# Gate products of a graph network in blocks: seven block multiplications in place of eight

## The chip, the cores and the metric

One core of one Trainium2 chip. The metric is the device time of one execution in microseconds (us), median. Executions of one kernel agree within about 0.2%. Ratios are the mean time of one kernel's fast runs over that of the kernel before in the same rounds, so they are not quite the ratio of the medians that are quoted.

## The reference

64 graphs of 256 nodes with 256 features, f32. Layer 0 is a normalisation with ReLU and three rounds of message passing with a gated (GRU) update; layer 1 is a graph attention. Cut to what matters:

```python
for i in range(3):
    m = h @ weight[i]
    aggr = A^T m                                # per graph
    gi = aggr @ w_ih.T + b_ih                   # three gates of 256 from 256
    gh = h    @ w_hh.T + b_hh
    r = sigmoid(i_r + h_r);  z = sigmoid(i_z + h_z)
    n = tanh(i_n + r * h_n)
    h = (1 - z) * n + z * h
x = x + h
# then, per graph: h1 = relu(norm(x)) @ W.T ; masked softmax of scores ; x = x + alpha @ h1
```

## The kernel before

Two graphs (a "pair") are worked on together, features on partitions, so that a gate operand is 2 x 128 features by 2 x 256 nodes = 512 columns. The products `weight[i] @ w_ih.T` are formed once (`gw`). A gate block of 128 outputs is then 2 or 4 multiplications of 128x128 by 128x512 into one result bank of PSUM:

```python
def gate(e, parts, ...):
    pg = Buf("bank")
    for part in parts:                 # "h": hidden state, "i": aggregate
        for kb in range(DB):           # two halves of the contraction
            w = whhT[:, kb, ts(e, P)] if part == "h" else gw[:, i, kb, ts(e, P)]
            nc.tensor.matmul(pg.t, w, feats(src)[:, kb, :], start=..., stop=...)
    ...
```

PSUM is the memory that TensorE writes its results to; SBUF is the working memory that all engines share. That makes 8 for r, 8 for z and 8 for n per layer: 24 wide multiplications. ScalarE applies sigmoid and tanh, VectorE the elementwise rest. The attention ends with a handover: TensorE transposes the softmax weights into PSUM ("turn"), VectorE copies them to SBUF, and TensorE multiplies ("mix"):

```python
pe(4 * TR, turn, ...)                                            # transposes
dve(V512, lambda: nc.vector.tensor_copy(pT.t[:, :GN], pt.t), ...)
pe(4 * MM, mix, ...)                                             # alpha @ h1
```

Every call of `pe`, `act`, `dve`, `pool` adds an operation with an assumed duration to a plan. A list scheduler in the kernel orders them: at each step it takes the operation that can start earliest by the assumed durations, then the one with the nearest deadline. At most three pairs are under way, and the deadline of pair p is 78 us x p in this kernel. The order that it finds is fixed for each engine; at run time an engine works through its own in sequence.

## Time and profile before

Median 2653.11 us (2652.37 to 2654.27). Busy shares of the span:

| engine | busy us | share |
|---|---|---|
| TensorE (PE) | 2613.3 | 99% |
| VectorE (DVE) | 1141.7 | 43% |
| ScalarE (ACT) | 1021.2 | 39% |
| GpSimd (POOL) | 251.0 | 9% |

A busy share is an upper bound on useful work: matmuls overlap, their ends are modelled, and the tail of one covers a short wait behind it. The cost of a matmul is its distance to the next start. In the page's groups the columns are the line, engine and operation, what is written and read, the shapes and the count, then busy us, mean ns of one, and idle time before it with its releaser. PE is TensorE's multiplications and PEld its weight loads, which are instructions of their own.

One more thing is seen in the chain in order of time (start us, length us, what). These are the first gate stretches of two pairs in a row:

```profile
228.03 20.85 PE bank L427 x48
...
309.07 20.84 PE bank L427 x48
```

A pair takes 309.07 - 228.03 = 81.04 us (81.03 over several).

### The profile page before, as it was taken

To read this page: it belongs to the slowest core of one execution; us is meant where nothing else is said; L and a number is where in the kernel's file an instruction comes from. 1 tells how busy PE (TensorE), PEld (TensorE's weight loads), DVE (VectorE), ACT (ScalarE), POOL (GpSimd) and SP (SyncE) were. 2 spreads that over 40 slices of the span, in tenths; PEclk is the share of its full clock that TensorE was granted. 3 is DMA by queue.
4 is the path that set the end of the run, shared out by engine and by line. 5 is a ranking of instruction groups with operands and counts; after the bars stand their busy time and mean duration, and the time that the engine had idled before them with its cause. 6 is when DMAs were issued, how large, how long until landed. Compare 5 with 4: busy or idle time off the path is not lost.

```text
span 2652.0 us, 23413 instructions
## 1 busy us (share of the span) xinstructions
PE 2613.3 (99%) x8929; PEld 1442.7 (54%) x8929; DVE 1141.7 (43%) x2341; ACT 1021.2 (39%) x1885; POOL 251.0 (9%) x294
## 2 busy tenths in 40 slices
PE   8999999999999999999999999999999999999997
PEld 5555555555555555555555545555555555455554
DVE  2444544344443445443444434354434444343433
ACT  3434443234443344432344433444323444334432
POOL 2101110101100011101011000111010110001000
PEclk9999999999999999999999999999999999999998
DMA  3000000000000000000000000000000000000000
GB/s 111 8 24 25 24 24 0 24 24 24 24 9 16 24 24 24 24 1 24 24 24 24 9 15 24 24 24 24 1 24 24 24 25 9 16 8 9 8 9 8
DMA packets 53520, 54.46 MB, mean 21 GB/s; under 512 B 1680, under 2 KB 53408, under 8 KB 53408
## 3 DMA queue, kind: packets, MB, share of 16 engines
q1 hardware_dynamic: 53376, 52.96, 6.0%
q8 instruction: 70, 1.15, 0.2%
q14 instruction: 42, 0.34, 0.0%
q10 hardware_dynamic: 32, 0.01, 0.0%
HBM read 36.18 MB, written 16.78 MB: 20 GB/s over the span
## 4 chain that ended last, share of the span: by engine, by line
PE 98%; DVE 1%; ACT 0%; DMA 0%; issue 0%; POOL 0%; ACTq 0%; DVEq 0%
PE bank L427 75%; PE bank L410 7%; PE bank L556 4%; PE bank L501 4%; PE bank L473 3%; PE bank L372 2%; DVE full L551 1%; PE bank L547 1%; PE bank L307 1%; PE bank L512 0%; PE bank L284 0%; DMA rows<-in_L_gnn_b_hh_dram 0%; ACT full L531 0%; DVE small L344 0%; ACT L531 0%
## 5 line engine op out<-in xcount | busy, mean ns | idle before, releaser
L427 PE MATMUL bank<-full,whhT 128*128 128x512 f32 x2304 | 1032.0, 593 | 0.0
L427 PE MATMUL bank<-full,gw 128*128 128x512 f32 x2304 | 1028.6, 593 | 0.0
L427 PEld LDWEIGHTS bank<-full,gw 128*128 128x128 f32 x2304 | 428.2, 190 | 515.1 <-issue 491.7
L427 PEld LDWEIGHTS bank<-full,whhT 128*128 128x128 f32 x2304 | 426.0, 190 | 474.2 <-issue 473.2
L444 DVE SCALAR_TENSOR_TENSOR full<-bank,vec,full 128x512 f32<-128x512 f32 x192 | 141.4, 749 | 562.2 <-ACT full L441 394.4
L449 ACT ACTIVATE full<-full,vec 128x512 f32<-128x512 f32 x192 | 138.5, 722 | 604.8 <-DVE full L448 604.8
L352 POOL TENSOR_TENSOR small<-small,nhalf 128x2 f32<-128x2 f32 x128 | 102.9, 821 | 2310.8 <-DVE small L350 2310.8
L448 DVE TENSOR_TENSOR full<-full,bank 128x512 f32<-128x512 f32 x192 | 131.3, 684 | 428.5 <-PE bank L427 428.5
L359 ACT ACTIVATE full<-x,small 128x256 f32<-128x256 f32 x256 | 139.3, 594 | 273.6 <-DVE small L354 273.6
L441 ACT ACTIVATE full<-bank,b_rz 128x512 f32<-128x512 f32 x192 | 131.9, 687 | 257.5 <-PE bank L427 257.5
L410 PE MATMUL bank<-round,round 128*128 128x256 f32 x1536 | 229.0, 302 | 0.0
L410 PEld LDWEIGHTS bank<-round,round 128*128 128x128 f32 x1536 | 195.6, 191 | 31.1 <-issue 30.6
L455 DVE TENSOR_TENSOR full<-full,full 128x512 f32<-128x512 f32 x192 | 132.5, 690 | 126.1 <-ACT full L449 126.1
L414 ACT COPY full<-bank 128x512 f32<-128x512 f32 x192 | 109.3, 589 | 154.2 <-PE bank L410 154.2
L452 ACT ACTIVATE full<-bank,b_rz 128x512 f32<-128x512 f32 x192 | 131.9, 687 | 71.6 <-PE bank L427 71.2
L457 DVE TENSOR_TENSOR full<-full,full 128x512 f32<-128x512 f32 x192 | 132.3, 689 | 20.1 <-ACT full L452 20.1
L458 DVE TENSOR_TENSOR full<-full,full 128x512 f32<-128x512 f32 x192 | 132.8, 692 | 6.6
L556 PE MATMUL bank<-full,full 128*128 128x256 f32 x512 | 119.6, 386 | 10.3 <-DVE full L551 10.3
L481 ACT CAST round<-bank 128x512 fp32r<-128x512 f32 x128 | 68.8, 589 | 153.5 <-PE bank L473 153.5
L501 PE MATMUL bank<-wT,full 128*128 128x258 f32 x512 | 117.8, 382 | 0.0
L483 DVE TENSOR_TENSOR round<-bank,round 128x512 fp32r<-128x512 f32 x128 | 81.6, 679 | 75.0 <-ACT round L481 75.0
L473 PEld LDWEIGHTS bank<-ident,full 128*128 128x128 f32 x768 | 90.9, 142 | 42.0 <-issue 34.6
(54 smaller groups left out, 1522.2 us busy)
## 6 DMA issues: line engine op xcount, KB each, us to landing
x<-in_x_dram SPq DMA_DIRECT2D x32, 512.0 KB, 4.8
adj<-in_adj_dram SPq DMA_DIRECT2D x32, 512.0 KB, 3.9
out_dram<-x SPq DMA_DIRECT2D x32, 512.0 KB, 2.8
full<-in_L_gnn_w_ih_dram SPq DMA_DIRECT2D x2, 384.0 KB, 5.9
full<-in_L_gnn_w_hh_dram SPq DMA_DIRECT2D x2, 384.0 KB, 6.8
full<-in_L_gnn_weight_dram SPq DMA_DIRECT2D x3, 256.0 KB, 6.6
full<-in_L_gnn_W_dram SPq DMA_DIRECT2D x1, 256.0 KB, 7.1
rows<-in_L_gnn_a_dram ACTq DMA_DIRECT2D x1, 2.0 KB
```

The source lines that it names most:

```text
L359: act(495, lambda k=k, nb=nb: nc.scalar.activation(nodes(dst)[:, k, :], nodes(src)[:, k, :], AF.Relu, bias=sm.t[:, 18 + nb : 19 + nb], sca ...
L410: nc.tensor.matmul(pa.t[:, ts(db, N)], nodes(part)[:, k, ts(db, P)], Ar()[:, k, :], start=(n == 0), stop=(n == len(terms) - 1))
L427: nc.tensor.matmul(pg.t, w, feats(src)[:, kb, :], start=(part == parts[0] and kb == 0), stop=(part == parts[-1] and kb == DB - 1))
L441: act(AB512, lambda pr=pr, ub=ub, er=er: nc.scalar.activation(ub(), pr.t, AF.Sigmoid, bias=b_rz[:, er : er + 1]), r=[(pr, ONE), ("b_rz", O ...
L444: dve(665, lambda ph=ph, ub=ub, en=en: nc.vector.scalar_tensor_tensor(ub(), ph.t, b_h[:, en : en + 1], ub(), op0=ALU.add, op1=ALU.mult), r ...
L449: act(630, lambda ub=ub, en=en: nc.scalar.activation(ub(), ub(), AF.Tanh, bias=b_i[:, en : en + 1]), r=[("vec", ONE)], w=[(u, q)])
L455: dve(V512, lambda d=d, ub=ub, db=db, hT=hT: nc.vector.tensor_sub(d(), feats(hT)[:, db, :], ub()), r=[(hT, q), (u, q)], w=[(hT_new, q)])
L457: dve(V512, lambda d=d, zb=zb: nc.vector.tensor_mul(d(), d(), zb()), r=[(z, q)], w=[(hT_new, q)])
L458: dve(V512, lambda d=d, ub=ub: nc.vector.tensor_add(d(), d(), ub()), r=[(u, q)], w=[(hT_new, q)])
L473: nc.tensor.transpose(pt.t[:, (nb * DB + db) * P : (nb * DB + db + 1) * P], feats(hT)[:, db, ts(g * NB + nb, P)], ident)
L501: nc.tensor.matmul(pm.t[:, : D + 2], quarters(hT)[:, db, g, ts(nb, P)], wT[:, db, :], start=(db == 0), stop=(db == DB - 1))
L556: nc.tensor.matmul(pv.t[:, ts(ib, D)], pT.t[:, (jb * NB + ib) * P : (jb * NB + ib + 1) * P], h1v()[:, g * NB + jb, :D], start=(jb == 0), s ...
```

## The change

The intent is to take TensorE work away. Weight and operand are each split into 2x2 blocks (output half by feature half; feature half by graph). The seven-product scheme replaces the eight block multiplications: with A the weight and B the operand,

S1 = A21+A22, S2 = S1-A11, S3 = A11-A21, S4 = A12-S2; T1 = B12-B11, T2 = B22-T1, T3 = B22-B12, T4 = T2-B21.

The weight sums are formed once in the setup (F11, F12, FS1 to FS4 in the code; FM22 is minus A22). The operand's sums are formed in each layer, on GpSimd for the hidden state and on VectorE for the aggregate. Three result banks X, Q, Z collect the products. X goes on accumulating after ScalarE has copied it out ("snapshot"), and VectorE adds Q or Z to the copies. Core of the diff, cut:

```diff
-    plan.slot_class("full", [... for i in range(20)])
+    plan.slot_class("full", [... for i in range(23)])
-    plan.slot_class("x", [... for i in range(WINDOW + 2)])
+    plan.slot_class("x", [... for i in range(WINDOW + 1)])
...
+        for sel in ("hh", "g"):
+            product(X, F11, ("B", B11), sel)
+            product(Q, F12, ("B", B21), sel)
+            product(Z, FS1, ("T", T1), sel)
+        snap(0, 0)                       # ScalarE copies X
+        add(0, 0, Q)                     # VectorE adds bank Q to the copy
+        ... product(X, FS2, ("T", T2), sel)
+        snap(0, 1)
+        ... product(X, FS3, ("T", T3), sel)
+        snap(1, 1)
+        add(1, 1, Z)
+        ... product(X, FM22, ("T", T4), sel);  product(Z, FS4, ("B", B22), sel)
+        add(0, 1, Z)
+        return X                         # X itself is the fourth block
...
+            Th = right_factors(nc.gpsimd, pool, hT)
+            Tg = right_factors(nc.vector, dve, agT)
+            Xrz = block_product([gates(0), gates(1)], RZ)
+            Xn = block_product([gates(2)[:1], gates(2)[1:]], U)
...
-        order = plan.run(lambda p: 78000.0 * max(p, 0))
+        order = plan.run(lambda p: 30000.0 * max(p, 0))
```

The last line makes the deadlines flatter, 30 us from pair to pair, so the scheduler mixes the pairs under way more freely.

More of the change, by code (lines that the diff above doesn't have):

```diff
@@ L185, in tile_gated_gnn_then_gat @@
     WIDE = NBLK * (D + 2)
-    plan.slot_class("full", [const.tile([P, WIDE], F32, name=f"full{i}") for i in range(20)])
+    plan.slot_class("full", [const.tile([P, WIDE], F32, name=f"full{i}") for i in range(23)])
     plan.slot_class("round", [const.tile([P, NBLK * D], F32R, name=f"round{i}") for i in range(9)])
-    plan.slot_class("x", [const.tile([P, NBLK * D], F32, name=f"x{i}") for i in range(WINDOW + 2)])
+    plan.slot_class("x", [const.tile([P, NBLK * D], F32, name=f"x{i}") for i in range(WINDOW + 1)])
     plan.slot_class("adj", [const.tile([P, NBLK * N], I32, name=f"adj{i}") for i in range(2)])
@@ L231, in tile_gated_gnn_then_gat @@
     b_h = vec[:, 2 * DB + EB :]
-    gw = const.tile([P, L, DB, E3], F32, name="gw")
-    whhT = const.tile([P, DB, E3], F32, name="whhT")
+    F11, F12, FS4, FM22, FS1, FS2, FS3 = range(7)
+    fac = {m: const.tile([P, 7, 3, P], F32, name=f"fac_{m}") for m in ("hh", 0, 1, 2)}
     wT = const.tile([P, DB, D + 2], F32, name="wT")
@@ L288, in transposed, with factors, sums, copies @@
                         dst(c)[:, r0 * P : (r0 + n) * P], pt.t[:, : n * P]), r=[(pt, ONE)], w=[region(c, r0)])
+        def factors(m, T):
+            blk = lambda eb, kb: T[kb].t[:, :E3].rearrange("p (s b e) -> p s b e", s=3, b=DB)[:, :, eb, :]
+            f = fac[m]
+            def sums():
+                nc.vector.tensor_add(f[:, FS1], blk(1, 0), blk(1, 1))
+                nc.vector.tensor_sub(f[:, FS2], f[:, FS1], blk(0, 0))
+                nc.vector.tensor_sub(f[:, FS3], blk(0, 0), blk(1, 0))
+                nc.vector.tensor_sub(f[:, FS4], blk(0, 1), f[:, FS2])
+                nc.vector.tensor_scalar(f[:, FM22], blk(1, 1), -1.0, None, op0=ALU.mult)
+            def copies():
+                nc.scalar.copy(f[:, F11], blk(0, 0))
+                nc.scalar.copy(f[:, F12], blk(0, 1))
+            r = [(T[kb], (0, 3)) for kb in range(DB)]
+            act(900, copies, r=r, w=[(f"fac{m}", (0,))])
+            dve(2200, sums, r=r, w=[(f"fac{m}", (1,))])
         whh_n = rows_of(w_hh, EB)
         load(0)
-        transposed(lambda c: whhT[:, c, :], lambda c, r0: ("whhT", ((c, r0),)), whh_n)
+        whhT = [Buf("full") for _ in range(DB)]
+        transposed(lambda c: whhT[c].t, lambda c, r0: (whhT[c], (r0,)), whh_n)
+        factors("hh", whhT)
         wih_n = rows_of(w_ih, EB)
@@ L299, in setup @@
             transposed(lambda c, w_T=w_T: feats(w_T)[:, c, :], lambda c, r0, w_T=w_T: (w_T, ((c, r0),)), w_n)
+            gT = [Buf("full") for _ in range(DB)]
             for db in range(DB):
@@ L310, in setup @@
                     pe(3 * MM, go, r=[(w_T, ((0, 0), (1, 0))), (wihT[0], (0, 3)), (wihT[1], (0, 3))], w=[(pg, ONE)])
-                    act(370, lambda i=i, db=db, sl=sl, pg=pg: nc.scalar.copy(gw[:, i, db, sl], pg.t[:, : E3 // 2]),
-                        r=[(pg, ONE)], w=[("gw", ((i, db, half),))])
+                    act(370, lambda b=gT[db], sl=sl, pg=pg: nc.scalar.copy(b.t[:, sl], pg.t[:, : E3 // 2]),
+                        r=[(pg, ONE)], w=[(gT[db], (3 * half,))])
+            factors(i, gT)
         W_n = rows_of(W, DB)
@@ L327, in setup, with right_factors, first @@
                 r=[(pl, ONE)], w=[("wT", (DB + db,))])
-    WHH = [("whhT", tuple((c, r0) for c in range(DB) for r0 in (0, 3)))]
     WT = [("wT", (0, 1, 2, 3))]
-    def gw_keys(i, e):
-        return [("gw", tuple((i, db, e // 3) for db in range(DB)))]
+    B11, B12, B21, B22 = range(4)
+    T1, T3, T2, T4 = range(4)
+    quarter = lambda b, q: b.t[:, q * N : (q + 1) * N]
+    def right_factors(eng, op, b):
+        T = Buf("full")
+        c = (1195, 605, 605) if eng is nc.gpsimd else (V512, V256, V256)
+        def first():
+            q = quarters(b)
+            eng.tensor_sub(T.t[:, : 2 * N].rearrange("p (c n) -> p c n", c=2), q[:, :, 1, :],
+                           b.t[:, : 2 * N].rearrange("p (c n) -> p c n", c=2))
+        op(c[0], first, r=[(b, (B11, B12, B22))], w=[(T, (T1, T3))])
+        op(c[1], lambda: eng.tensor_sub(quarter(T, T2), quarter(b, B22), quarter(T, T1)),
+           r=[(b, (B22,)), (T, (T1,))], w=[(T, (T2,))])
+        op(c[2], lambda: eng.tensor_sub(quarter(T, T4), quarter(T, T2), quarter(b, B21)),
+           r=[(b, (B21,)), (T, (T2,))], w=[(T, (T4,))])
+        return T
@@ new lines, in block_product, with product, go, snap @@
+    def block_product(halves, dest):
+        X, Q, Z = Buf("bank"), Buf("bank"), Buf("bank")
+        both = lambda b: b.t.rearrange("p (s n) -> p s n", s=2)
+        started = set()
+        def product(bank, f, right, sel):
+            terms = [(s, t) for s in range(2) for t in halves[s] if t[0] == sel or (sel == "g" and t[0] != "hh")]
+            if not terms:
+                return
+            first = bank not in started
+            started.add(bank)
+            kind, q = right
+            srcs = lambda t: t[2] if kind == "B" else t[3]
+            def go():
+                for n, (s, t) in enumerate(terms):
+                    nc.tensor.matmul(bank.t[:, ts(s, N)], fac[t[0]][:, f, t[1], :], quarter(srcs(t), q),
+                                     start=(first and n == 0), stop=True, skip_group_check=True)
+            pe(MM * len(terms), go, r=[(srcs(t), (q,)) for _, t in terms] + [(f"fac{t[0]}", (0, 1)) for _, t in terms],
+               w=[(bank, ONE)])
+        def snap(e, g):
+            act(A512, lambda: nc.scalar.copy(quarters(dest[e])[:, :, g, :], both(X)), r=[(X, ONE)], w=[(dest[e], (g, 2 + g))])
+        def add(e, g, bank):
+            dve(V512, lambda: nc.vector.tensor_add(quarters(dest[e])[:, :, g, :], quarters(dest[e])[:, :, g, :], both(bank)),
+                r=[(bank, ONE)], w=[(dest[e], (g, 2 + g))])
+        for sel in ("hh", "g"):
[4 more added lines that the diff above has]
+        add(0, 0, Q)
+        for sel in ("hh", "g"):
+            product(X, FS2, ("T", T2), sel)
+        snap(0, 1)
+        for sel in ("hh", "g"):
+            product(X, FS3, ("T", T3), sel)
+        snap(1, 1)
+        add(1, 1, Z)
+        for sel in ("hh", "g"):
+            product(X, FM22, ("T", T4), sel)
+            product(Z, FS4, ("B", B22), sel)
+        add(0, 1, Z)
+        return X
@@ L416, in pair @@
                     r=[(pa, ONE)], w=[(agT, (g, G + g))])
-            def gate(e, parts, i=i, hT=hT, agT=agT):
-                pg = Buf("bank")
-                for part in parts:
-                    src = hT if part == "h" else agT
-                    def go(part=part, src=src):
-                        for kb in range(DB):
-                            w = whhT[:, kb, ts(e, P)] if part == "h" else gw[:, i, kb, ts(e, P)]
-                            nc.tensor.matmul(pg.t, w, feats(src)[:, kb, :],
-                                             start=(part == parts[0] and kb == 0),
-                                             stop=(part == parts[-1] and kb == DB - 1))
-                    pe(4 * MM, go, r=[(src, ALL)] + (WHH if part == "h" else gw_keys(i, e)), w=[(pg, ONE)])
-                return pg
@@ L434, in pair @@
-            hT_new, u, z = Buf("full"), Buf("full"), Buf("full")
+            Tg = right_factors(nc.vector, dve, agT)
+            RZ, U = [Buf("full") for _ in range(DB)], [Buf("full") for _ in range(DB)]
+            gates = lambda s: [("hh", s, hT, Th), (i, s, agT, Tg)]
+            Xrz = block_product([gates(0), gates(1)], RZ)
+            Xn = block_product([gates(2)[:1], gates(2)[1:]], U)
+            act(A512, lambda U=U, Xn=Xn: nc.scalar.copy(quarters(U[1])[:, :, 0, :], Xn.t.rearrange("p (s n) -> p s n", s=2)),
+                r=[(Xn, ONE)], w=[(U[1], (0, 2))])
@@ new lines, in pair @@
+            for s in range(2):
+                act(630, lambda s=s, RZ=RZ: nc.scalar.activation(
+                    feats(RZ[0])[:, s, :], feats(RZ[0])[:, s, :], AF.Sigmoid, bias=b_rz[:, 2 * s : 2 * s + 1]),
+                    r=[("b_rz", ONE)], w=[(RZ[0], (2 * s, 2 * s + 1))])
+                act(370, lambda s=s, RZ=RZ, X=Xrz: nc.scalar.activation(
+                    quarter(RZ[1], 2 * s), X.t[:, ts(s, N)], AF.Sigmoid, bias=b_rz[:, 2 * s + 1 : 2 * s + 2]),
+                    r=[("b_rz", ONE), (Xrz, ONE)], w=[(RZ[1], (2 * s,))])
+                act(370, lambda s=s, RZ=RZ: nc.scalar.activation(
+                    quarter(RZ[1], 2 * s + 1), quarter(RZ[1], 2 * s + 1), AF.Sigmoid, bias=b_rz[:, 2 * s + 1 : 2 * s + 2]),
+                    r=[("b_rz", ONE)], w=[(RZ[1], (2 * s + 1,))])
@@ L435, in pair @@
             for db in range(DB):
-                er, ez, en = db, DB + db, 2 * DB + db
+                en = 2 * DB + db
+                u = lambda b=U[db]: feats(b)[:, 0, :]
+                d = lambda db=db, hT=hT: feats(hT)[:, db, :]
                 q = (2 * db, 2 * db + 1)
-                ub = lambda db=db, u=u: feats(u)[:, db, :]
-                zb = lambda db=db, z=z: feats(z)[:, db, :]
-                pr = gate(er, "hi")
-                act(AB512, lambda pr=pr, ub=ub, er=er: nc.scalar.activation(
-                    ub(), pr.t, AF.Sigmoid, bias=b_rz[:, er : er + 1]), r=[(pr, ONE), ("b_rz", ONE)], w=[(u, q)])
@@ L443, in pair @@
-                ph = gate(en, "h")
-                dve(665, lambda ph=ph, ub=ub, en=en: nc.vector.scalar_tensor_tensor(
-                    ub(), ph.t, b_h[:, en : en + 1], ub(), op0=ALU.add, op1=ALU.mult),
-                    r=[(ph, ONE), ("vec", ONE)], w=[(u, q)])
-                pn = gate(en, "i")
-                dve(V512, lambda pn=pn, ub=ub: nc.vector.tensor_add(ub(), ub(), pn.t), r=[(pn, ONE)], w=[(u, q)])
-                act(630, lambda ub=ub, en=en: nc.scalar.activation(
-                    ub(), ub(), AF.Tanh, bias=b_i[:, en : en + 1]), r=[("vec", ONE)], w=[(u, q)])
@@ L451, in pair @@
-                pz = gate(ez, "hi")
-                act(AB512, lambda pz=pz, zb=zb, ez=ez: nc.scalar.activation(
-                    zb(), pz.t, AF.Sigmoid, bias=b_rz[:, ez : ez + 1]), r=[(pz, ONE), ("b_rz", ONE)], w=[(z, q)])
-                d = lambda db=db, b=hT_new: feats(b)[:, db, :]
-                dve(V512, lambda d=d, ub=ub, db=db, hT=hT: nc.vector.tensor_sub(d(), feats(hT)[:, db, :], ub()),
-                    r=[(hT, q), (u, q)], w=[(hT_new, q)])
-                dve(V512, lambda d=d, zb=zb: nc.vector.tensor_mul(d(), d(), zb()), r=[(z, q)], w=[(hT_new, q)])
@@ L458, in pair @@
-                dve(V512, lambda d=d, ub=ub: nc.vector.tensor_add(d(), d(), ub()), r=[(u, q)], w=[(hT_new, q)])
-            hT = hT_new
+                dve(660, lambda u=u, db=db, en=en, RZ=RZ: nc.vector.scalar_tensor_tensor(
+                    u(), u(), b_h[:, en : en + 1], feats(RZ[db])[:, 0, :], op0=ALU.add, op1=ALU.mult),
+                    r=[(RZ[db], (0, 1)), ("vec", ONE)], w=[(U[db], (0, 1))])
+                dve(V512, lambda u=u, b=U[db]: nc.vector.tensor_add(u(), u(), feats(b)[:, 1, :]),
+                    r=[(U[db], (2, 3))], w=[(U[db], (0, 1))])
@@ new lines, in pair @@
+                act(630, lambda u=u, en=en: nc.scalar.activation(u(), u(), AF.Tanh, bias=b_i[:, en : en + 1]),
+                    r=[("vec", ONE)], w=[(U[db], (0, 1))])
+                dve(V512, lambda u=u, d=d: nc.vector.tensor_sub(d(), d(), u()), r=[(U[db], (0, 1))], w=[(hT, q)])
+                dve(V512, lambda d=d, b=RZ[db]: nc.vector.tensor_mul(d(), d(), feats(b)[:, 1, :]),
+                    r=[(RZ[db], (2, 3))], w=[(hT, q)])
+                dve(V512, lambda u=u, d=d: nc.vector.tensor_add(d(), d(), u()), r=[(U[db], (0, 1))], w=[(hT, q)])
```

## The prediction

> **What bounds the kernel now.** I read the page first: the busy shares, the 40 slices, the chain that ended last and the costliest groups. The chain in order of time came next, then the busy time by stretches and single rows of the timeline.
>
> ```profile
> PE 2613.3 (99%) x8929; PEld 1442.7 (54%) x8929; DVE 1141.7 (43%) x2341; ACT 1021.2 (39%) x1885; POOL 251.0 (9%) x294
> PE 98%; DVE 1%; ACT 0%; DMA 0%; issue 0%; POOL 0%; ACTq 0%; DVEq 0%
> L427 PE MATMUL bank<-full,whhT 128*128 128x512 f32 x2304 | 1032.0, 593 | 0.0
> L427 PE MATMUL bank<-full,gw 128*128 128x512 f32 x2304 | 1028.6, 593 | 0.0
> ...
> L448 DVE TENSOR_TENSOR full<-full,bank 128x512 f32<-128x512 f32 x192 | 131.3, 684 | 428.5 <-PE bank L427 428.5
> ```
>
> TensorE sets the end: 98% of the chain lies on it, and the three other compute engines are idle for more than half of the span. The gate products (L427) are 4608 instructions. The program has 24 multiplications per layer and pair of graphs, times 96, which is 2304: each f32 multiplication is two instructions. Their mean of 593 ns is a latency, not a cost, since neighbours overlap. The cost is start to start, which the chain in order of time gives:
>
> ```profile
> 147.26 20.60 PE bank L427 x48
> 174.08 20.60 PE bank L427 x48
> ...
> 1248.01 0.87 PE bank L473 x8
> 1248.88 6.87 PE bank L427 x16
> ...
> 1258.34 3.49 PE bank L501 x16
> ...
> 1268.30 1.91 PE bank L410 x16
> ```
>
> Wide gate instruction (512 columns): 20.60/48 = 429.2 ns. The projection has 258 columns, f32, with a fresh weight load each: 3.49/16 = 218.1 ns. So 256 columns should take about 216.5 ns, and one load per 216 ns is hidden. A transpose is 0.87/8 = 109 ns, a propagation 1.91/16 = 119 ns. This pace gives the gates 4608 x 0.4292 = 1978 us; all of TensorE's work at such paces sums to about 2596 us, so about 56 us of the span is idle or drain. Where that is:
>
> ```profile
> 0.00:66.00 66.00, 55.54 (x200) 33.06 (x201) 16.43 (x44) 25.80 (x50) 14.59 (x21) 1.00 0.33 112
> 66.00:2500.00 2434.00, 2423.91 (x8314) 1337.36 (x8313) 1067.73 (x2189) 947.71 (x1746) 233.72 (x269) 1.00 0.06 19
> 2500.00:2571.00 71.00, 69.46 (x219) 36.46 (x218) 30.64 (x57) 25.34 (x46) 1.34 (x2) 1.00 0.00 1
> 2571.00:2652.00 81.00, 64.37 (x201) 35.85 (x198) 26.86 (x52) 22.38 (x43) 1.34 (x2) 0.89 0.04 13
> ```
>
> (First number the length, second TensorE's busy time.) The ramp loses 10 us, the long middle only 10 us in 2434, the last 81 us about 17. The rest of the 56 is drain that counts as busy. The steady state is wholly bound by TensorE.
>
> **What the Trainium skill says.** "TensorE: Matmul & The Clock Gate", section Back-to-back issue gap, gives N/2.4 + 2.5 ns for a warm matmul. The trace agrees if each f32 instruction makes two passes: 2 x 512/2.4 + 2.5 = 429.2, exactly what is seen, and 2 x 258/2.4 + 2.5 = 217.5 against 218.1. So halving the columns costs almost nothing per column here: two narrow instructions take 433.0 against 429.2. "PSUM — Partial Sum Buffer", section The four PSUM rules, says that hardware allows a synchronised read of a partial sum in the middle of an accumulation group; the change rests on it, and no trace of the kernel before shows it. "VectorE: DVE Perf Modes", section The TRN2 errata, gives (N+151)/0.96 ns for an f32 two-tensor operation: 691 at 512, as measured (medians of 692 on L455, L457 and L458), and so 424 at 256. "SBUF — State Buffer", section 🔬 SBUF: two separate sides, says that VectorE with two SBUF inputs and GpSimd lock each other out for a whole instruction. L396 on GpSimd reads 1265/1270/1300 ns min/median/max, so there was no such collision before; there can be now.
>
> **The change part by part**, per layer and pair (96 of them).
>
> Removed from TensorE: 24 wide multiplications become 6 products x 7 x 256 columns = 42 narrow ones; the built order confirms 4032 of them in all. 42 x 2 x 0.2165 = 18.19 us against 24 x 2 x 0.4292 = 20.60. Saved 2.41 us, x96 = 232 us. If nothing else moved, the time would be 2653 - 232 = 2421 us.
>
> Added on VectorE: six additions from PSUM at 684 ns (4.10 us) and the sums of the aggregated operand, one of 512 columns and two of 256 (0.69 + 2 x 0.42 = 1.54). 5.64 x 96 = 542 us, and about 11 us of weight sums in the setup. 1142 becomes 1695, which is 69% of a span of 2450.
>
> Added on ScalarE: seven snapshots and copies out of PSUM at 589 ns (the L414 kind): 4.12 us. The four sigmoids of 687 ns (2.75 us) become two from SBUF at about 722, two half-width from PSUM at about 475 and two half-width from SBUF at 498: 3.39. Sum 4.76 x 96 = 457 us; 1021 becomes 1478, 60%.
>
> Added on GpSimd: sums of the hidden state, 1.27 + about 2 x 0.64 = 2.55, x96 = 245 us; 251 becomes 496, 20%.
>
> None of the additions is TensorE's own work, and no engine rises above TensorE's 96%. What of it reaches the path is waits. A result bank is read by ScalarE and then accumulated further, so the next multiplication into it has to wait for the snapshot. After the last multiplication of a group that is 0.16 us of drain beyond its slot, 0.59 us of copy and two handovers of 0.05 (0.04 to 0.05 in the timeline): about 0.86 us, if ScalarE is free. In the built order I counted the TensorE work laid between the two accesses for the 429 places that show a ScalarE wait on a bank in mid-use: at least 0.96 us, 1.7 us or more in 335, median 2.2. So the order covers every snapshot, but 94 have at most some 0.8 us to spare, and ScalarE, 60% busy in strict order, will sometimes be late. I charge 0.1 us for each of the 672 snapshots and copies: 67 us if none of it is absorbed; I take half to three quarters, 30 to 50 us, an estimate and not a measurement.
>
> Ramp: the weight products now come ahead of the first gate work, and each set needs two copies (2 x 0.48) and five sums of 384 columns (5 x 0.56 = 2.8, from the VectorE formula). I charge 5 us over the old 10. Tail: before, the last pair runs its last two layers alone. The new order interleaves the last pairs more closely (products of two pairs alternate until about the last layer), which should return a few us, while the lone last layer now has a longer chain of snapshots and additions. I set it to zero net. The x buffers fall from 5 to 4 and the general ones rise from 20 to 23; the inputs land in about 5 us and are asked for two pairs ahead, so I charge nothing.
>
> Sum: 2653 - 232 + 5 + 24 to 44 = 2450 to 2470; I choose 2455.
>
> **The rivals.** (1) Waits for the snapshots and additions eat most of the gain: three banks per block product, up to two products per pair-layer, in eight banks with several pairs alive. For it: 69% and 60% busy engines working in strict order, and more waits in TensorE's order (1705 rows carry one against 1358). Against it: the spacing of 0.96 us or more, and that the same kind of static order lost only 0.4% in the middle of the kernel before. If each of the 672 cost 0.3 us, 200 us would come back and the time would be about 2620. (2) GpSimd and VectorE lock each other out: 8.5 us of two-input SBUF work per layer on VectorE against 2.55 us on GpSimd. For it: the skill's page. Against it: both have idle time, and an overlap chance of about a third x 2.55 us is under 1 us per layer and mostly off TensorE's path. It would add 0 to 40 us. (3) Weight loads show up: twice as many loads per streamed column. Against it: 218.1 ns at 258 columns with a load each. If they cost 10 ns each, 8064 x 0.010 = 81 us, a time of about 2530. (4) The waits vanish altogether and the closer interleaving also hides the old waits: TensorE's new work is 2596 - 232 = 2364, plus 40 of ramp and tail, about 2405.
>
> **Range and chances.** The floor of the range is rival 4, the top is rival 3 or half of rival 1: 2405 to 2530. Faster by over 2% means under 2600; only a full rival 1 or two rivals together miss it. Faster 0.94, within 2% 0.05, slower 0.01.
>
> **What would show it.** Right: 8064 gate instructions at about 216 ns start to start, PE busy near 2400 us, VectorE near 1700, ScalarE near 1480, GpSimd near 500, the chain still above 90% on TensorE, and idle before the gate products of some tens of us, released by ScalarE. Wrong: a pace of 225 ns or more (rival 3); chain shares on ScalarE or VectorE of 5% and up, or idle of over 100 us before the gate matmuls (rival 1); GpSimd sums well above 1.3 us or VectorE's two-input rows above 692 ns (rival 2). A busy sum of VectorE far above 1700 would mean that I missed work.

## The result, and the profile after

Median 2404.19 us (2403.07 to 2405.30, four runs) against 2652.74 in the same rounds: ratio 0.9062, 95% interval 0.9046 to 0.9078. That is just under the lower end of the predicted range (2405) and 51 us under the predicted 2455. From the page after, its busy line and the share of the chain by engine:

```profile
PE 2366.8 (99%) x12385; PEld 2097.8 (87%) x12385; DVE 1671.0 (70%) x3225; ACT 1412.9 (59%) x2757; POOL 536.2 (22%) x582
PE 96%; DVE 2%; ACT 1%; issue 0%; DMA 0%; POOL 0%; ACTq 0%; DVEq 0%; POOLq 0%
```

TensorE still sets the end. The added busy time of the others is near what the prediction worked out (1695, 1478 and 496). The chain in order of time, after, two successive pairs:

```profile
199.01 11.22 PE bank L404 x52
214.30 5.61 PE bank L404 x26
...
271.81 11.22 PE bank L404 x52
```

A 256-column gate instruction is 5.61/26 = 215.8 ns start to start, and a pair takes 271.81 - 199.01 = 72.80 us. The idle time before the gate products, by releaser (us in all, times). This view adds the wait of a weight load to that of the multiplication behind it, although the two overlap:

```profile
its engine sat idle before it (us, times) until:
  DVE full L552: 7.3, 4
  ACT full L411: 2.6, 2
  DVE full L376: 0.4, 2
```

So of the 2.6 us for the 576 snapshots (L411), 1.5 are one weight load's wait and 1.1 that of the multiplication behind it, in one place: TensorE waited for a snapshot once. Ramp, middle and tail after (length, then TensorE's busy time):

```profile
0.00:66.00 66.00, 55.54 (x265) 44.23 (x266) 31.49 (x69) 33.91 (x68) 22.06 (x29) 0.97 0.32 104
66.00:2320.00 2254.00, 2250.78 (x11845) 2004.22 (x11844) 1594.68 (x3066) 1342.03 (x2613) 508.66 (x546) 1.00 0.06 21
2320.00:2402.30 82.30, 60.51 (x279) 49.32 (x277) 44.87 (x92) 36.95 (x78) 5.44 (x7) 0.87 0.04 13
```

The ramp idles as long as before (10.5 us), the middle 3 us of 2254, the tail 22 of 82 us (17 of 81 before).

**Where 250 us went.** Thirty-two pairs at the old period are 2593.0 us of a span of 2652.0; at the new one they are 2329.6 of 2402.3. So the periods gave 263.4 us and the ramp and tail took back 13.7. Of the 263.4, the gate products are 4608 x 0.4292 - 8064 x 0.2158 = 237.5 us. The other 25.9 us, 0.8 per pair, are not in the pace of the products. The chain shows most of it at the handover to the mix. Before:

```profile
216.88 0.45 PE bank L547 x4
217.33 0.02 issue
217.35 0.70 DVE full L551
218.05 0.04 issue
218.10 3.72 PE bank L556 x16
```

The chain leaves TensorE for VectorE's copy, and the mix itself takes 3.72 us. After:

```profile
248.65 0.87 PE bank L640 x8
249.52 0.43 PE bank L404 x2
249.96 0.94 PE bank L512 x8
250.90 0.86 PE bank L404 x4
251.76 3.45 PE bank L649 x16
```

The chain stays on TensorE, because other work lies between the transposes and the mix, and the mix takes 3.45. In these two extracts, transposes, handover and mix take 4.93 us before, and transposes and mix 4.32 after: 0.6 us of the 0.8. In the order that the traces show there is no other work between transposes and mix in 31 of 32 pairs before, and in 30 of 32 pairs 6 gate instructions and 8 of propagation, about 2.2 us, after. The other 0.2 us per pair is a short wait in the wide gate products, which run 3 shows.

### The profile page after: what moved, and what is told of

It reads as the page before. It is cut to its first block, busy times and chain, and to the rows that moved or that the text cites. A ratio compares the mean times of both kernels' runs of the same rounds, so it can differ in the third digit from the quotient of the medians.

```text
span 2402.3 us, 32347 instructions
## 1 busy us (share of the span) xinstructions
PE 2366.8 (99%) x12385; PEld 2097.8 (87%) x12385; DVE 1671.0 (70%) x3225; ACT 1412.9 (59%) x2757; POOL 536.2 (22%) x582
## 4 chain that ended last, share of the span: by engine, by line
PE 96%; DVE 2%; ACT 1%; issue 0%; DMA 0%; POOL 0%; ACTq 0%; DVEq 0%; POOLq 0%
PE bank L404 72%; PE bank L512 7%; PE bank L649 5%; PE bank L594 4%; PE bank L566 4%; PE bank L473 2%; PE bank L640 1%; PE bank L605 1%; PE bank L335 0%; DVE full L552 0%; DVE full L549 0%; DVE small L445 0%; DVE full L550 0%; DVE full L542 0%; ACT full L624 0%
## 5 line engine op out<-in xcount | busy, mean ns | idle before, releaser
L404 PE MATMUL bank<-full,fac 128*128 128x256 f32 x4032 | 1015.2, 379 | 0.0
L404 PE MATMUL bank<-full,fac_hh 128*128 128x256 f32 x4032 | 988.8, 379 | 4.5 <-DVE full L552 3.4
L404 PEld LDWEIGHTS bank<-full,fac 128*128 128x128 f32 x4032 | 752.0, 190 | 95.1 <-DVE full L376 0.4
L404 PEld LDWEIGHTS bank<-full,fac_hh 128*128 128x128 f32 x4032 | 746.5, 190 | 96.8 <-DVE full L552 3.9
L414 DVE TENSOR_TENSOR full<-full,bank 128x512 f32<-128x512 f32 x576 | 386.3, 685 | 419.2 <-PE bank L404 400.2
L411 ACT COPY full<-bank 128x512 f32<-128x512 f32 x576 | 332.9, 584 | 331.7 <-PE bank L404 331.7
L372 POOL TENSOR_TENSOR full<-full 128x512 f32<-128x512 f32 x96 | 124.4, 1296 | 1146.4 <-DVE full L552 1085.0
L528 ACT ACTIVATE full<-full,b_rz 128x512 f32<-128x512 f32 x192 | 135.2, 721 | 222.6 <-DVE full L414 222.6
L512 PE MATMUL bank<-round,round 128*128 128x256 f32 x1536 | 249.1, 305 | 1.7 <-DVE round L576 1.7
L512 PEld LDWEIGHTS bank<-round,round 128*128 128x128 f32 x1536 | 209.7, 190 | 12.0 <-DVE round L576 1.9
L460 ACT ACTIVATE full<-x,small 128x256 f32<-128x256 f32 x256 | 142.4, 594 | 59.1 <-DVE small L455 59.1
L542 DVE SCALAR_TENSOR_TENSOR full<-full,vec,full 128x512 f32<-128x512 f32 x192 | 135.5, 747 | 2.7
L550 DVE TENSOR_TENSOR full<-full,full 128x512 f32<-128x512 f32 x192 | 131.2, 696 | 4.4
L516 ACT COPY full<-bank 128x512 f32<-128x512 f32 x192 | 109.9, 573 | 32.8 <-PE bank L512 32.8
L552 DVE TENSOR_TENSOR full<-full,full 128x512 f32<-128x512 f32 x192 | 124.6, 689 | 0.1
L545 DVE TENSOR_TENSOR full<-full 128x512 f32<-128x512 f32 x192 | 123.6, 684 | 0.0
L372 DVE TENSOR_TENSOR full<-full 128x512 f32<-128x512 f32 x96 | 66.6, 694 | 81.6 <-ACT full L516 81.6
```

Of the source, the lines that this page charges most:

```text
L372: eng.tensor_sub(T.t[:, : 2 * N].rearrange("p (c n) -> p c n", c=2), q[:, :, 1, :], b.t[:, : 2 * N].rearrange("p (c n) -> p c n", c=2))
L404: nc.tensor.matmul(bank.t[:, ts(s, N)], fac[t[0]][:, f, t[1], :], quarter(srcs(t), q), start=(first and n == 0), stop=True, skip_group_che ...
L411: act(A512, lambda: nc.scalar.copy(quarters(dest[e])[:, :, g, :], both(X)), r=[(X, ONE)], w=[(dest[e], (g, 2 + g))])
L414: dve(V512, lambda: nc.vector.tensor_add(quarters(dest[e])[:, :, g, :], quarters(dest[e])[:, :, g, :], both(bank)), r=[(bank, ONE)], w=[(d ...
L460: act(495, lambda k=k, nb=nb: nc.scalar.activation(nodes(dst)[:, k, :], nodes(src)[:, k, :], AF.Relu, bias=sm.t[:, 18 + nb : 19 + nb], sca ...
L512: nc.tensor.matmul(pa.t[:, ts(db, N)], nodes(part)[:, k, ts(db, P)], Ar()[:, k, :], start=(n == 0), stop=(n == len(terms) - 1))
```

## The experiments

In the diffs of this section code is cut. The theory to test (A): the scheduler's order pays for a part of the result; it hides the snapshots altogether and, beyond that, hides the handover that the old order exposed. Its rivals: the extra gain comes from the products or buffers themselves; the snapshots do cost what the prediction charged; lockouts between GpSimd and VectorE matter.

**1. The kernel before with the flat slope alone.**

```diff
-        order = plan.run(lambda p: 78000.0 * max(p, 0))
+        order = plan.run(lambda p: 30000.0 * max(p, 0))
```

> The kernel before with only the scheduler's deadline slope taken from the change (30 us per pair in place of 78 us); the built order now lays 3.4 us of gate products between the softmax transposes and the multiplication that needs them, in 31 of 32 pairs, where it had none. Theory A (part of the gain is the order, which hides the handover to the softmax multiplication): period per pair falls from 81.04 to about 80.2 us, time about 2630 us, within 8 us. Theory B (the order gives nothing, all of the gain is the seven products): 2652 us, within 4 us.

Measured 2631.91 us, ratio 0.9921 (0.9905 to 0.9938). The handover in its chain:

```profile
234.37 0.88 PE bank L547 x8
235.25 3.43 PE bank L427 x8
238.68 3.45 PE bank L556 x16
```

Gate products now lie between the two, and the chain no longer touches VectorE. Twenty-one of the 250 us can be had without any block product. The period falls from 81.03 to 80.47 us, which is 18 of the 21; 0.33 us per pair over the sum of the paces (80.14) stay. Theory A holds for the handover.

**2. The changed kernel with the old steep slope** (the same line the other way round).

> The changed kernel with the old slope of 78 us per pair; the built order now lays only 0.4 to 0.9 us of work between the softmax transposes and their multiplication. Theory A: some of the handover comes back, 0.2 to 0.6 us per pair or 6 to 20 us, time 2410 to 2424 us. Theory B: 2404 us within 4 us. If snapshots need the interleaving that the flat slope gives, waits of over 100 us before the gate products and a time above 2500 us.

Measured 2510.61 us, ratio 0.9465 (0.9451 to 0.9479). Theory A's direction is right, but the size is five times its upper figure: the steep slope costs the changed kernel 106 us. The time lies above the 2500 us that I had set for snapshots that need the flat slope. Idle before its gate products:

```profile
  DVE full L552: 17.7, 20
  DVE full L372: 16.9, 21
  DVE full L376: 16.7, 28
  DVE full L414: 11.5, 29
  ACT full L411: 10.6, 28
...
```

These waits are many and mostly on VectorE, along the elementwise steps, not on the snapshots. But the longest in total are elsewhere, at the transposes and the propagation (engine, line, what was waited for: us, times, longest):

```profile
PE bank L473 <- ACT full L460: 24.3, 34, 4.6
PE bank L512 <- DVE round L576: 12.2, 10, 1.9
```

L460 is ScalarE's step of the normalisations. In the changed kernel these two are 6.4 and 1.7 us. Run 12 follows the snapshots up.

**3. The kernel before with 256-column gate multiplications**, still eight per block:

```diff
-    nc.tensor.matmul(pg.t, w, feats(src)[:, kb, :], start=..., stop=...)
+    for g in range(G):
+        nc.tensor.matmul(pg.t[:, ts(g, N)], w, quarters(src)[:, kb, g, :], start=..., stop=...)
```

> The kernel before with each gate multiplication of 512 columns given as two of 256 with their own weight loads, eight block multiplications in all, nothing else. Theory A: 9216 gate instructions at 215.8 ns in place of 4608 at 429.2, plus 11 us, time about 2664 us. Rival (weight loads show when a load serves 256 columns only): 225 ns each, time above 2740 us.

Measured 2657.23 us, ratio 1.0015 (1.0000 to 1.0030), 4.7 us more where 11 were expected. Its longest chain pieces read:

```profile
147.33 20.72 PE bank L428 x96
```

That is 215.8 ns for one, as assumed. A period in it is (985.67 - 742.25)/3 = 81.14 us, 0.11 above the kernel before, where the paces alone ask for 288 x 0.2158 - 144 x 0.4292 = 0.35. The missing 0.24 per pair is about the difference between 20.85 and 20.60 us for the same 48 wide instructions in the kernel before: a short wait in one stretch, which the narrow form does not show. The trace of the kernel before names it, a weight load that waits for ScalarE's copy of the aggregate:

```profile
PEld bank L427 <- ACT full L414: 22.6, 28, 0.8
```

Run 1 still has it (23.4 us), run 3 does not. Weight loads are hidden: twice as many per column cost 0.3% at most (the upper end of the interval).

**4. Each snapshot copied twice**, in the same order, the scheduler not told:

```diff
-    act(A512, lambda: nc.scalar.copy(quarters(dest[e])[:, :, g, :], both(X)), ...)
+    def twice():
+        nc.scalar.copy(quarters(dest[e])[:, :, g, :], both(X))
+        nc.scalar.copy(quarters(dest[e])[:, :, g, :], both(X))
+    act(A512, twice, ...)
```

> The changed kernel with every one of the 576 snapshots copied twice by ScalarE, in the same static order, results right. It adds 576 x about 0.48 = 276 us to ScalarE (59% to some 70%) and 0.48 us to the time that each result bank is held. Theory A (the order lays so much work between the accesses that the snapshots cost nothing): under 25 us more, 2404 to 2430 us. Rival (the snapshots were just covered, and a late one stalls TensorE in full): up to 276 us more, and at least 60 us.

Measured 2483.00 us, ratio 0.9363 (0.9349 to 0.9377): 79 us more than the changed kernel, so theory A's number missed and the rival's lower bound held. Idle before the gate products:

```profile
  ACT full L413: 140.8, 244
  DVE full L556: 7.3, 4
...
```

(L413 is the second copy.) Taken apart, the 140.8 us are

```profile
PEld bank L404 <- ACT full L413: 93.0, 152, 1.8
PE bank L404 <- ACT full L413: 47.8, 92, 1.4
```

A snapshot later than the scheduler believed does stall TensorE: 152 weight loads waited, and 92 multiplications. The 79 us lie between the two sums. So the snapshots are covered, but with little to spare.

**5. The same doubled snapshots, told to the scheduler** as 0.475 us more:

```diff
-    act(A512, twice, ...)
+    act(A512 + 475, twice, ...)
```

> The snapshots copied twice as in the run before, but the scheduler is told so (0.95 us in place of 0.475), so the order is made for it. The extra work on ScalarE is the same 276 us. Theory A (what a snapshot costs is decided by whether the static order lays enough TensorE work behind it): most of the 79 us goes, time 2405 to 2430 us. Rival (ScalarE's load itself holds TensorE back): about 2480 us again.

Measured 2439.44 us, ratio 0.9195 (0.9181 to 0.9208). With the same extra work on ScalarE, 44 of the 79 us are gone, but 35 stay, more than expected. They are not waits for snapshots: idle before the gate products for L413 is down from 140.8 to 6.6 us. TensorE's longest wait is now at the propagation, for a VectorE step, about once per pair (in the changed kernel that wait, at L512, is 1.7 us in all):

```profile
PE bank L516 <- DVE round L580: 24.1, 30, 1.8
```

One thing that the scheduler still had wrong can be read from ScalarE's timeline (start, length):

```profile
1201.66 0.60 ACT L412 COPY full<-bank 128x512 f32<-128x512 f32 x1
1202.29 0.59 ACT L413 COPY full<-bank 128x512 f32<-128x512 f32 x1
1202.78 0.51 ACT L538 ACTIVATE full<-full,b_rz 128x256 f32<-128x256 f32 x1
```

The second copy starts 0.63 us after the first, probably because it writes the same place and waits for it, while the next instruction follows the second copy after 0.49. The scheduler had been told 0.475 for each. That these 0.15 us lead to the wait at the propagation is not shown.

**9. The same again, with the right figure.** `A512 + 620`.

> As the run with the doubled snapshots that the scheduler knows of, but told 0.62 us for the second copy, which is what it took (the second waits for the first, so it starts 0.62 us later and not 0.475). ScalarE's extra work is the same. Theory A (the order decides, and what was left was the 0.14 us that the scheduler did not know of): 2405 to 2420 us. Rival (ScalarE at some 70% costs TensorE time whatever the order): 2435 to 2445 us as before.

Measured 2420.98 us, ratio 0.9129 (0.9116 to 0.9143), 1 us over the upper end of the expected span. Idle before the gate products:

```profile
  DVE full L418: 21.9, 58
  ACT full L413: 1.7, 2
...
```

In this view the waits for snapshots have gone from 140.8 us to 1.7, although ScalarE copies exactly as much as in run 4, and the wait at the propagation from 24.1 to 1.8. Some 17 us stay; the trace has 21.9 us of weight-load waits for VectorE's additions (L418). What a snapshot costs thus depends on whether the order was made for its duration, and not on ScalarE's load alone; that the order finds room for all of it is not assured, as the 17 us show.

**6. No additions.** VectorE's 576 additions from PSUM are left out, in the same order. The result is wrong (relative error 0.38).

```diff
-    dve(V512, lambda: nc.vector.tensor_add(dest.., dest.., both(bank)), ...)
+    dve(V512, lambda: None, ...)
```

> The changed kernel without the 576 VectorE additions from PSUM (results wrong on purpose: the sums of products are left out), in the same static order. VectorE's busy time falls by about 386 us to 1290. Theory A (the additions lie beside TensorE's work): at most 10 us less, 2394 to 2404 us, and that from the lone tail. Rival (part of the additions is on the path): 2370 us or less.

Measured 2399.62 us, ratio 0.9046 (0.9031 to 0.9061). VectorE's busy time fell from 1671 to 1326 us and the time by 4.6: the additions lie beside TensorE's work.

**10. No snapshots.** No multiplication into a result bank waits for a snapshot any more; the additions become plain copies of the second bank. Wrong (relative error 0.43).

```diff
-    act(A512, lambda: nc.scalar.copy(quarters(dest[e])[:, :, g, :], both(X)), ...)
+    act(A512, lambda: None, ...)
-    nc.vector.tensor_add(dest.., dest.., both(bank))
+    nc.vector.tensor_copy(dest.., both(bank))
```

> The changed kernel without ScalarE's 576 snapshots, the additions being plain copies of the second bank (results wrong on purpose), so no multiplication into a result bank waits for ScalarE any more; same static order. Theory A (the snapshot waits cost nothing as the order stands): 2404 us within 6 us, the gain in the lone tail alone. The prediction's charge for late snapshots: 30 to 50 us less, 2354 to 2374 us.

Measured 2402.97 us, ratio 0.9060 (0.9045 to 0.9075): 1.2 us less than the changed kernel, within the spread. The 576 snapshots cost nothing that can be measured. This is the cleanest answer to the prediction's charge for late snapshots.

**7. Narrow multiplications and flat slope together**, in the kernel before: eight block multiplications in the change's grain and under its slope (edits of runs 1 and 3).

> The kernel before with 256-column gate multiplications and the flat deadline slope, so eight block multiplications in the change's grain and under its scheduling. Theory A: the two single effects add up, 2632 + 5 = 2637 us, within 6 us; from there seven in place of eight is worth 1152 instructions x 215.8 ns = 249 us, which would leave 2388, and the changed kernel's 2404 says that its added work costs some 16 us. Rival (the grain and the order interact): outside 2625 to 2650 us.

Measured 2634.65 us, ratio 0.9929 (0.9914 to 0.9944). The effects add up. Against this kernel the changed one has 1152 gate instructions fewer, worth 1152 x 0.2158 = 249 us, and is 230 us faster: the seven-product scheme gives back 18 us in all for its added work, its longer tail included. The chain says where. Two first gate stretches in a row in this run:

```profile
572.02 20.72 PE bank L428 x96
652.54 20.72 PE bank L428 x96
```

The period is 80.52 us, and the paces ask for 80.49, so slope and narrow form together remove nearly all of the old loss per pair. The changed kernel's 72.80 is 7.72 less, where 36 instructions at 0.2158 are worth 7.77. In the steady state the added work thus costs 0.05 us per pair, under 2 us in all; the other 16 or so are ramp and tail.

**8. The hidden state's sums on VectorE** instead of GpSimd.

```diff
-            Th = right_factors(nc.gpsimd, pool, hT)
+            Th = right_factors(nc.vector, dve, hT)
```

> The changed kernel with the hidden state's sums moved from GpSimd to VectorE: GpSimd's busy time falls by some 290 us to about 250, VectorE rises by about 148 us to 1820 (76%). Theory A (lockouts between GpSimd and VectorE exist but are off the path): 2404 us within 8 us, and the longest VectorE two-input rows come back from 1.1 to 1.7 us to 0.7 us. Rival 2 of the prediction (lockouts on the path): 10 to 40 us faster. Rival (VectorE at 76% becomes late): over 2415 us.

Measured 2402.15 us, ratio 0.9053 (0.9039 to 0.9066): no difference that counts. GpSimd was indeed slowed in the changed kernel. Its two 256-column sums, minimum/median/maximum ns:

```profile
L376 POOL TENSOR_TENSOR full<-full,full x96: 722/734/1087, 16.8 to 2342.0; 128x256 f32<-128x256 f32 x96
...
L378 POOL TENSOR_TENSOR full<-full,full x96: 721/727/1296, 17.6 to 2342.8; 128x256 f32<-128x256 f32 x96
```

The longest are 570 ns over the median, but no wait of TensorE is put down to them. VectorE's busy time rose by 92 us and not by 148. The second half of the expectation missed: two VectorE rows (L550, L552) still have maxima of 1642 and 1637 ns in this run. The traces show why. In the kernel before no VectorE operation takes over 800 ns; in the changed kernel 69 do, and in run 8 four, all within 4 us, beside GpSimd's splitting of the state at the start of a pair (L495, L497). Of the 69, four are of that kind and three belong to the setup; 59 of the rest are two steps, one of the normalisation (L455) and one of the masking (L615), that meet GpSimd's sums about once per pair. One of them, minimum/median/maximum ns in the changed kernel and then in run 8:

```profile
L455 DVE SCALAR_TENSOR_TENSOR small<-small x128: 129/160/1246, 8.7 to 2378.5; 128x2 f32<-128x2 f32 x128
L455 DVE SCALAR_TENSOR_TENSOR small<-small x128: 128/154/539, 8.6 to 2377.0; 128x2 f32<-128x2 f32 x128
```

So the sums do hold VectorE up, and the time does not show it.

**11. The old buffer counts** in the changed kernel (20 and 5 in place of 23 and 4).

> The changed kernel with the old buffer counts, 20 general tiles in place of 23 and 5 for x in place of 4. Theory A (buffers do not bind under the flat slope): 2404 us within 5 us. Rival (the three tiles are part of the gain): over 2415 us.

Measured 2404.62 us, ratio 0.9066 (0.9052 to 0.9079): the buffers are no part of the gain.

**12. Steep slope and no snapshots** (edits of runs 2 and 10; wrong).

> The steep slope of 78 us per pair and no snapshots, additions given as plain copies (results wrong on purpose): what made the steep order 106 us slower. If the snapshot waits did, most of it goes: 2404 to 2440 us. If the elementwise chains of pairs that stand too close together did (the trace of the steep order has its gate products idle for VectorE as much as for ScalarE), at least two thirds stay: 2475 us or more.

Measured 2498.08 us, ratio 0.9420 (0.9404 to 0.9436). Of the 106 us that the steep slope costs, 94 stay without any snapshot. So it is not the snapshots that need the flat slope. That it is the chains of steps on VectorE and ScalarE in pairs that stand too close is what the waits of run 2 suggest (TensorE's wait for the normalisation is 24.8 us here, 24.3 there); no run takes those chains away, and the cause of the 94 us stays open.

No run beat the changed kernel by more than its spread. The 4.6 us of run 6 are not a version, since its result is wrong.

## Why the prediction was right or wrong

**Right.** TensorE as the bound before and after; 4032 narrow multiplications; weight loads hidden (rival 3 falls, run 3); lockouts off the path as far as the hidden state's sums go (rival 2, run 8), though its signs, VectorE rows above 692 ns and GpSimd sums above 1.3 us, did appear at their longest (1662 and 1599 ns); additions beside TensorE's work (run 6); no snapshot waits of the size of rival 1 as the order stands. The buffers weighed nothing (run 11).

**Wrong: the charge for late snapshots.** The step that failed reads "I charge 0.1 us for each of the 672 snapshots and copies: 67 us if none of it is absorbed; I take half to three quarters, 30 to 50 us". (The sum then wrote 24 to 44, a slip of mine.) The runs show 1.2 us (run 10), and the trace one wait of 1.1 to 1.5 us. I argued from ScalarE's average share, 60% busy and "sometimes late". But the order is static and was made with ScalarE's queue in it, so its share of busy time does not say how often a snapshot is late; the count of work behind each snapshot does. My count of at least 0.96 us behind each snapshot was the right reading, and I then overruled it. The worry itself was not baseless: 0.6 us of unforeseen delay per snapshot costs 79 us (run 4), and telling the scheduler removes 62 of them (run 9). Nor are known durations enough: the order of run 2 was made with the same ones and loses 106 us.

**Wrong: the loss in the old order.** "The ramp loses 10 us, the long middle only 10 us in 2434" was read off the busy time, and I wrote that the rest of the 56 us was drain. It was not all drain. The period of 81.03 us against the paces' sum (61.80 for the gates, 5.73 propagation, 5.67 transposes, 3.49 projection, 3.45 mix: 80.14) shows 0.9 us lost per pair, 28 us in all; after, the same sum is 72.72 of 72.80. I had named the possibility as rival 4 and left it out of the sum. Run 1 measures it: 21 us, 18 of them in the period, from the slope alone; most of the rest is the short wait in the wide gate products, which goes with the narrow form (run 3).

**Off in size.** Narrow pace 215.8 instead of 216.5 ns: 8064 x 0.0007 = 6 us more gain. (The formula that the prediction cites gives 215.8; I took 216.5 from the 258-column pace.) GpSimd's 256-column sums take 0.73 us undisturbed (means 0.84 and 0.90), not 0.64. Ramp and tail took back 13.7 us in place of the 5 that I charged. By the busy times the ramp idles as long as before and the tail 5 us longer, where TensorE waits 6.8 us at a stretch for VectorE after the last gate product of the last pair. Where the other 9 us lie is not settled, and no run tests it. The four terms add up to the miss: about 29 us charged for snapshots that cost next to nothing, 26 lost in the old order and now gone, 6 of pace, less 9 of ramp and tail, are 52 us, against the 51 between 2455 and 2404.

The predicted floor of 2405, "about", was rival 4: no waits and the old ones hidden. That is what happened, but that its sum (2364 + 40) comes out right to a microsecond is luck. It starts from 2596 us of TensorE work, for which I showed no sum; the counts of the page times the paces give about 2585, so that 67 us and not 56 were idle or drain. At the measured pace the new work is 2585 - 238 = 2347 us, and 55 us stand beside it in place of 40: the two errors cancel. I gave this rival too little weight.

## What to carry to other kernels

When one engine is the bound in a statically ordered kernel, compare the period of the steady state with the sum of start-to-start paces; busy time hides small losses behind modelled ends. Added work on idle engines can be nearly free where the order was made with its duration: the same copies cost 79 us unforeseen and 17 us foreseen. It is not free by that alone: under the steep slope, with the same durations, the kernel lost 106 us. A change that comes with a scheduling constant should be split into the two before the gain is credited: the slope was worth 21 us without the products and 106 us with them.

## What the Trainium skill lacked or had wrong

- "Trainium Kernel Development and Optimization", section Performance Expectations, calls matmul busy time a bad metric, and MFU (the share of peak arithmetic) and LDWEIGHTS busy share good ones. The first half is borne out: TensorE reads 99% busy both before and after, with 0.9 us lost per pair before. For LDWEIGHTS the second half is not borne out here: weight loads went from 54% to 87% busy in run 3 by halving the columns, and the kernel became 0.15% slower.
- "TensorE: Matmul & The Clock Gate", section Back-to-back issue gap, has no row for f32, and no page gives a gap in ns for it. Here one f32 multiplication is two instructions of 429.2 ns at 512 columns and 215.8 at 256, which is 2N/2.4 + 2.5 each; the page's remark that the formula over-counts at large N does not hold for them.
- "SBUF — State Buffer", section 🔬 SBUF: two separate sides, states the lock between GpSimd and VectorE. The runs agree that operations grow (727 ns median, 1296 at most on GpSimd; 69 operations over 800 ns on VectorE, four once the sums are off GpSimd). What the page does not give is what that costs a kernel: here moving the sums changed the time by 2 us in 2404.
- No page covers what a read in the middle of an accumulation costs. Here 576 such reads of about 0.58 us cost 1.2 us in all, where the prediction had counted at least 0.96 us of TensorE work laid behind each of the 429 places that it looked at.
